# Reciprocal roots by bits and Newton steps on VectorE in a two-layer decoder, in place of ScalarE's square root

## The chip, the cores and the metric

The kernel runs on one core of a Trainium2 chip. Its time is the device time of that core in microseconds (us), the median of several executions. One further execution is recorded by the hardware profiler; all durations of single instructions come from there.

The engines are called PE (TensorE, matrix products), DVE (VectorE), ACT (ScalarE, functions from tables), POOL (GpSimd) and SP (SyncE, which here only issues transfers). Each works through its own queue of instructions in order.

## The reference

The input x has 4 batches of 512 tokens of 256 channels (2,048 tokens). Two layers follow one another, and each sublayer adds its output to x. What matters here:

- Layer 0: a layer norm, a causal convolution of four taps, then a mixer with 16 heads. Its query/key values are multiplied by a decay and a cosine of position, and divided by `max(sqrt(sum(qk * qk)), 1e-12)`, the sum going over a head's channels for each token; gated values are accumulated over the tokens (a running sum), multiplied back, projected, and layer-normed once more. Then cross-attention over the second input `ctx_768` with 16 heads, then a gate that chooses experts for each token, and the experts.
- Layer 1: an element-wise gated recurrence, a cross-attention block whose linear maps are quantised to whole numbers by maxima over the whole tensor, and a feed-forward part.

Every layer norm is `(x - mean) / sqrt(var + 1e-5)` over 256 channels. The reciprocal square root of that variance, and that of the head norms, are what the change touches.

## The kernel before, in words

A tile is 128 tokens; a batch has 4 tiles (QT = 4), and work goes batch by batch (b = 0 to 3). The kernel has two paths, chosen by what the data are; one runs, and the other stays behind a branch. The executed path goes through these stages:

- `l0_mixers`: the mixer of layer 0 and its cross-attention, interleaved. For a batch the mixer's steps are `normalize` (layer norm), `mix` (the convolution, L743 to L746), `measure` (query/key products, copies and squares on ACT at L756 and L758, sums), `scale`, `scale_near` and `scale_far` (the head norms), `factor` (fetch the factors for one group of heads), `gated_values`, `recall` (L821 is its end on DVE), `emit` (the projection `o`) and `absorb` (the second norm, and the addition to x). The cross-attention runs in 16 units, four a batch; a unit has eight `exponents`: PE makes scores, DVE takes maxima (L914), ACT makes the exponents (L917), which `gather` multiplies with the values. In the course of a batch's units the mixer's steps of the next batch are woven in.
- `l0_gate`, `l0_experts`: the choice of experts and the experts.
- `l1_attn`, `l1_xattn` (fuse, then the hidden block), `l1_ffn`: layer 1. `fold` products of weights for the last stage are put among the earlier ones, and its products `y` end the kernel.

What sets the order: a framework plans the instructions of every engine from the order in which the program gives them and from what each depends on, and it may put one ahead of another on the same engine; it adds the semaphores. What is given through `pinned` (matmuls, L579) or `move` (transfers on SP, L586) keeps the order of the program. Buffers come from pools with a fixed number for each name; a step whose buffer is still in use waits.

ACT holds one table of functions at a time. Where the next function is not in it, a table load (`ACT_TABLE_LOAD` in the profile) stands before the instruction, and is listed under its line.

The places that the change and the steps of the prediction touch:

- `rstd` (L154 to L168): the reciprocal root for the layer norms, on a tile of 128 partitions x 4 values. It adds the epsilon on DVE (L158), takes the root on ACT (L160), inverts on DVE (L162), and does one Newton step on DVE (L164 to L168). `normed` calls it, and so do `absorb` and the norms of the other stages: 28 times on the executed path (four each in `normalize`, the cross-attention's `tokens`, `absorb`, the gate, layer 1's recurrence, its fuse block and its feed-forward part).
- `scale_near` (L777 to L785): the head norms of a batch, laid out as 128 x 64: maximum with 1e-24 on DVE (L781), root on ACT (L782), reciprocal on DVE (L783), and two products with `near_dec` (L784, L785). Four times. Its input is fetched by SP from a buffer in memory (`rn<-far_ss`), its output goes back there (`far<-rn`), and from there to `factors`.
- `cosines` (L702 to L717): angles on DVE (L708 to L712), sine and square on ACT (L714, L715), and the product with the decays on POOL (L716, L717). The decays are powers built by doubling on DVE (L680 to L682), stored, and fetched again by SP as `near_dec` (used at L687 to L690) and as `decay`.
- The queue of SP at the start holds, in this order: weights and x, `far_dec<-dec` (2), `near_dec<-far_dec` (2), `decay<-far_dec` (16), `far_ss<-sums`, `rn<-far_ss`, `far<-rn` (2), `factors<-far`.

Of the kernel before, what the change touches and what calls it, by code (L numbers as in the profile page):

```python
# [9 lines left out]
F32 = mybir.dt.float32  # L10
F32R = mybir.dt.float32r
BF16 = mybir.dt.bfloat16
I32 = mybir.dt.int32
AF = mybir.ActivationFunctionType
ALU = mybir.AluOpType
# [3 lines left out]
P = 128  # L19
# [7 lines left out]
EPS = 1e-5  # L27
# [5 lines left out]
TWO_PI_INV = 0.15915494309189535  # L33

MAGIC = 12582912.0
FLT_MAX = 3.4028234663852886e38
CLAMP = 10000.0


class Kernel:  # L40


    def __init__(self, ctx, tc, a, out):
# [30 lines left out]
        self.magic = self.const.tile([P, 1], F32, name="magic")  # L74
        nc.gpsimd.memset(self.magic, MAGIC)

# [74 lines left out]
        return self.ps2.tile([P, 2, 512], F32, tag="pair", name=name)  # L151


    def rstd(self, var, n, pool):  # L154

        nc = self.nc
        v = pool.tile([P, n], F32, tag="ln_v", name="ln_v")
        nc.vector.tensor_scalar_add(v, var, EPS)  # L158
        s = pool.tile([P, n], F32, tag="ln_s", name="ln_s")
        nc.scalar.activation(s, v, AF.Sqrt)  # L160
        y = pool.tile([P, n], F32, tag="ln_y", name="ln_y")
        nc.vector.reciprocal(y, s)  # L162
        u = pool.tile([P, n], F32, tag="ln_u", name="ln_u")
        nc.vector.tensor_mul(u, y, y)  # L164
        nc.vector.tensor_mul(u, u, v)
        nc.vector.tensor_scalar(u, u, -0.5, 1.5, ALU.mult, ALU.add)
        r = pool.tile([P, n], F32, tag="ln_r", name="ln_r")
        nc.vector.tensor_mul(r, y, u)  # L168
        return r

    def moments(self, srcs, pool):

# [366 lines left out]
def l0_mixers(k):  # L539
# [18 lines left out]
    nc, tc, a = k.nc, k.tc, k.a  # L558
    k.close_psum()
    with ExitStack() as es:  # L560
        pool = lambda n, bufs, **kw: es.enter_context(tc.tile_pool(name=n, bufs=bufs, **kw))
        wp, wk, sp = pool("l0_w", 1), pool("l0", 2), pool("l0_s", 3)
# [214 lines left out]
        def scale_near(b):  # L777
            rn = near_of[b] = wk.tile([P, 3, 64], F32, tag="rn", name=f"rn_{b}", bufs=1)
            move(rn[:, 2, :], near(factors[b]))

            nc.vector.tensor_scalar_max(rn[:, 2, :], rn[:, 2, :], 1e-24)  # L781
            nc.scalar.activation(rn[:, 2, :], rn[:, 2, :], AF.Sqrt)  # L782
            nc.vector.reciprocal(rn[:, 2, :], rn[:, 2, :])  # L783
            nc.vector.tensor_mul(rn[:, 0, :], rn[:, 2, :], near_dec[:, 1, :])  # L784
            nc.vector.tensor_mul(rn[:, 1, :], rn[:, 2, :], near_dec[:, 0, :])  # L785

# [321 lines left out]
        for u in range(units + 1):  # L1108
            b, m = divmod(u, 4)
# [927 lines left out]
```

## Time and profile before

| | before |
|---|---|
| median of 3 runs | 1335.3 us (1335.01 to 1341.83) |
| profiled execution | 1344.59 us, span 1342.9 us |
| mean granted clock of PE | 0.847 of full speed |
| instructions | 11,723 |
| PE busy | 1002.3 us, 75% of the span |
| PE weight loads (beside PE) | 550.3 us, 41% |
| DVE busy | 789.0 us, 59%, 1,813 instructions |
| ACT busy | 454.5 us, 34%, 748 instructions |
| POOL busy | 205.5 us, 15% |

Busy time by stretch of the span, in us, as the trace gives it:

| stretch | work in it | PE | DVE | ACT | POOL |
|---|---|---|---|---|---|
| 0 to 32 | first norm, convolution, query/key | 15.9 | 16.7 | 8.1 | 9.0 |
| 32 to 62 | cosines, decays, head norms of batch 0 | 25.3 | 20.3 | 14.1 | 12.9 |
| 62 to 100 | factors of batch 0, `recall` | 10.0 | 20.7 | 4.1 | 9.6 |
| 100 to 157 | first units | 56.2 | 29.2 | 21.1 | 6.8 |
| 157 to 555 | layer 0's mixer and cross-attention | 287.6 | 277.5 | 228.3 | 62.4 |
| 555 to 900 | gate, experts, folds | 259.8 | 146.5 | 52.2 | 60.5 |
| 900 to 1105 | layer 1's recurrence, first part of its cross-attention | 147.5 | 117.9 | 64.9 | 42.2 |
| 1105 to 1343 | hidden block, feed-forward part | 200.1 | 160.3 | 61.9 | 2.3 |

An engine's busy time tells how much work it has; whether it holds others up is seen from the waits. A group of instructions is listed as line, engine, operation, what it writes and reads with the shape, and how often; after a bar its busy time and the mean duration of one in ns; after another the idle time of its engine before it and what ended most of that. The timeline lists single instructions by their start.

### The profile page before, as it was taken

To read this page: it belongs to the slowest core of one execution; us is meant where nothing else is said; L and a number is where in the kernel's file an instruction comes from. 1 tells how busy PE (TensorE), PEld (TensorE's weight loads), DVE (VectorE), ACT (ScalarE), POOL (GpSimd) and SP (SyncE) were. 2 spreads that over 40 slices of the span, in tenths; PEclk is the share of its full clock that TensorE was granted. 3 is DMA by queue.
4 is the path that set the end of the run, shared out by engine and by line. 5 is a ranking of instruction groups with operands and counts; after the bars stand their busy time and mean duration, and the time that the engine had idled before them with its cause. 6 is when DMAs were issued, how large, how long until landed. Compare 5 with 4: busy or idle time off the path is not lost. (4 is left out here: it accounts for less than half of the span.)

```text
span 1342.9 us, 11723 instructions
## 1 busy us (share of the span) xinstructions
PE 1002.3 (75%) x3734; PEld 550.3 (41%) x3734; DVE 789.0 (59%) x1813; ACT 454.5 (34%) x748; POOL 205.5 (15%) x224
## 2 busy tenths in 40 slices
PE   5729759767956867467199999948883688769997
PEld 1315332232413313156077577836442344245443
DVE  5565577578587666345136851145565656886564
ACT  2404437537555565310011421102341344741000
POOL 2321012112112101015300000071113110000000
PEclk9859869868977878766599999979996899878999
DMA  4264722343541322044575354173000011001000
GB/s 131 69 186 153 239 70 95 120 132 103 169 143 58 117 72 69 19 148 146 175 260 164 110 206 130 50 247 127 0 0 4 17 47 32 0 28 36 16 31 19
DMA packets 92344, 132.27 MB, mean 98 GB/s; under 512 B 21312, under 2 KB 62784, under 8 KB 92256
## 3 DMA queue, kind: packets, MB, share of 16 engines
q1 hardware_dynamic: 86768, 113.58, 27.0%
q0 software_dynamic: 5504, 17.83, 3.7%
q8 instruction: 32, 0.52, 0.2%
q14 instruction: 40, 0.33, 0.1%
HBM read 88.72 MB, written 42.66 MB: 98 GB/s over the span
## 5 line engine op out<-in xcount | busy, mean ns | idle before, releaser
L917 ACT ACTIVATE e<-score,tops 128x512 f32<-128x512 f32 x256 | 161.3, 687 | 144.1 <-DVE tops L914 79.9
L914 DVE TENSOR_REDUCE tops<-score 128x2 f32<-128x1024 f32 x128 | 155.5, 1219 | 61.9 <-PE score L579 61.7
L210 PE MATMUL y<-folded_sb,fht 128*128 128x512 f32 x256 | 113.4, 604 | 0.0
L952 PE MATMUL av<-e,weighed 128*32 128x512 f32 x512 | 86.0, 742 | 33.1 <-POOL weighed L940 33.1
L579 PE MATMUL score<-query,key 64*128 64x512 f32 x256 | 75.2, 586 | 43.7 <-ACT e L917 43.2
L1893 DVE SCALAR_TENSOR_TENSOR x_sb<-y,tt_w,x_sb 128x256 f32<-128x256 f32 x128 | 61.9, 483 | 39.2 <-PE y L210 35.9
L579 PEld LDWEIGHTS score<-query,key 64*128 64x128 f32 x256 | 27.7, 214 | 136.6 <-ACT e L917 83.9
L210 PE MATMUL ef<-sw,eact 128*128 128x256 f32 x320 | 80.2, 391 | 1.6 <-DVE ey L1411 1.6
L579 PE MATMUL o<-o_wT_sb,qk 128*128 128x256 f32 x128 | 43.2, 494 | 49.1 <-DVE qk L821 39.6
L210 PE MATMUL ef<-eht,sw 128*128 128x320 f32 x256 | 74.6, 435 | 0.6 <-ACT eact L1400 0.6
L210 PEld LDWEIGHTS y<-folded_sb,fht 128*128 128x128 f32 x256 | 49.3, 194 | 60.4 <-issue 60.4
L210 PE MATMUL fold<-w_out,w_in 128*128 128x256 f32 x256 | 69.7, 432 | 5.5 <-DMA w_out<-in_w_outT 5.5
L210 PEld LDWEIGHTS ef<-sw,eact 128*128 128x128 f32 x320 | 59.3, 195 | 12.5 <-DVE ey L1411 4.9
L210 PEld LDWEIGHTS fold<-w_out,w_in 128*128 128x128 f32 x256 | 55.1, 221 | 14.3 <-issue 5.9
L210 PEld LDWEIGHTS ef<-eht,sw 128*128 128x128 f32 x256 | 47.6, 190 | 18.4 <-ACT eact L1400 1.6
L579 PEld LDWEIGHTS o<-o_wT_sb,qk 128*128 128x128 f32 x128 | 30.0, 248 | 61.2 <-DVE qk L821 44.9
L1400 ACT ACTIVATE eact<-ef 128x640 f32<-128x640 f32 x32 | 22.4, 703 | 94.8 <-PE ef L210 94.7
L579 PE MATMUL xo<-Wo_sb,att 128*128 128x256 f32 x128 | 37.0, 438 | 16.8 <-POOL att L993 16.8
L210 PE MATMUL f<-aht,W_fT_sb 128*128 128x512 f32 x96 | 45.8, 620 | 2.8 <-DVE up L1511 1.4
L940 POOL TENSOR_TENSOR weighed<-v,weighed 128x256 f32<-128x256 f32 x16 | 10.9, 682 | 237.7 <-ACT weighed L939 237.7
L1435 POOL DMA_INDIRECT got<-table,rows x32 | 31.1, 972 | 105.1 <-DMA table<-ey 94.1
L1380 PE MATMUL eturn<-ident,rows 128*128 128x128 f32 x80 | 16.6, 291 | 34.7 <-DMA rows<-table 30.7
(372 smaller groups left out, 1803.8 us busy)
## 6 DMA issues: line engine op xcount, KB each, us to landing
table<-zeros POOLq DMA_DIRECT2D x8, 1152.0 KB
factors<-far SPq DMA_DIRECT2D x64, 128.0 KB
key<-far_k SPq DMA_DIRECT2D x16, 512.0 KB
query<-far_q SPq DMA_DIRECT2D x16, 512.0 KB
w_in<-in_w_in SPq DMA_DIRECT2D x8, 1024.0 KB
w_out<-in_w_outT SPq DMA_DIRECT2D x8, 1024.0 KB
rows<-table SPq DMA_DIRECT2D x8, 640.0 KB
table<-ey SPq DMA_DIRECT2D x8, 640.0 KB
```

The costliest lines, as they stand in the source:

```text
L210: self.nc.tensor.matmul(out, lhs_t, rhs, start=(i == 0), stop=(i == len(pairs) - 1))
L579: nc.tensor.matmul(out, lhs_t, rhs, start=start and i == 0, stop=stop and i == len(pairs) - 1)
L914: nc.vector.tensor_reduce(top, ps, AX.X, ALU.max, negate=True)
L917: nc.scalar.activation(e[:, i, :], ps[:, i, :], AF.Exp, bias=top[:, i : i + 1])
L940: weighing[0] = nc.gpsimd.tensor_mul(wt[:, :, :, 0:16], vs[u], wt[:, :, :, 16:17].to_broadcast([P, QT, 4, 16]),)
L952: nc.tensor.matmul(avs[u][32 * h : 32 * h + 32, :], weighed[u % 2][:, j, h, :], es_of[u, h // 2, j][:, h % 2, :], start=(j == 0), stop=(j ...
L1380: nc.tensor.transpose(ps[:, c, :], rows[:, i, c * P : (c + 1) * P], k.ident)
L1400: nc.scalar.activation(act[:, f, :].rearrange("p (j t) -> p j t", j=2), ps[:, :, :half], AF.Silu)
L1435: nc.gpsimd.indirect_dma_start(out=got, out_offset=None, in_=k.table, in_offset=bass.IndirectOffsetOnAxis(ap=k.rows[:, which, t : t + 1], ...
L1893: nc.vector.scalar_tensor_tensor(xt, ps[:, e, :], w[:, i, e4 + e : e4 + e + 1], xt, ALU.mult, ALU.add)
```

## The change

`rstd` no longer calls ACT. It computes half of (variance + epsilon) in one DVE instruction and hands it to a new helper, `inverse_root`. This takes a first guess from the bits of the float: one DVE instruction reads the half as a whole number, multiplies by -0.5 and adds a constant, and writes the whole number whose bits are the guess. The constant sets the sign bit too, so that the guess is negative. Three Newton steps follow, of three DVE instructions each: y times y, times the half, and (u - 1.5) times y, which flips the sign each time, so that after three steps it is positive. `rstd` has thus 11 DVE instructions in place of 6 and one on ACT.

`scale_near` does the same on its 128 x 64 tile: half of the maximum with 1e-24, then `inverse_root` in place, 11 DVE instructions in place of a maximum, ACT's root and a reciprocal. The two products with `near_dec` stay. Two small tiles are new.

```diff
+ROOT_BITS = float(0x5F3759DF - (1 << 22) - (1 << 31))

+    def inverse_root(self, y, half, u):
+        nc = self.nc
+        nc.vector.tensor_scalar(y.bitcast(I32), half.bitcast(I32), -0.5, ROOT_BITS, ALU.mult, ALU.add)
+        for _ in range(3):
+            nc.vector.tensor_mul(u, y, y)
+            nc.vector.tensor_mul(u, u, half)
+            nc.vector.scalar_tensor_tensor(y, u, 1.5, y, ALU.subtract, ALU.mult)
+
     def rstd(self, var, n, pool):
-        nc = self.nc
-        v = pool.tile([P, n], F32, tag="ln_v", name="ln_v")
-        nc.vector.tensor_scalar_add(v, var, EPS)
-        s = pool.tile([P, n], F32, tag="ln_s", name="ln_s")
-        nc.scalar.activation(s, v, AF.Sqrt)
-        y = pool.tile([P, n], F32, tag="ln_y", name="ln_y")
-        nc.vector.reciprocal(y, s)
-        u = pool.tile([P, n], F32, tag="ln_u", name="ln_u")
-        nc.vector.tensor_mul(u, y, y)
-        nc.vector.tensor_mul(u, u, v)
-        nc.vector.tensor_scalar(u, u, -0.5, 1.5, ALU.mult, ALU.add)
-        r = pool.tile([P, n], F32, tag="ln_r", name="ln_r")
-        nc.vector.tensor_mul(r, y, u)
-        return r
+        half, y, u = (pool.tile([P, n], F32, tag=f"ln_{t}", name=f"ln_{t}") for t in ("half", "y", "u"))
+        self.nc.vector.tensor_scalar(half, var, EPS, 0.5, ALU.add, ALU.mult)
+        self.inverse_root(y, half, u)
+        return y

     def scale_near(b):
-            nc.vector.tensor_scalar_max(rn[:, 2, :], rn[:, 2, :], 1e-24)
-            nc.scalar.activation(rn[:, 2, :], rn[:, 2, :], AF.Sqrt)
-            nc.vector.reciprocal(rn[:, 2, :], rn[:, 2, :])
+            half, u = (sp.tile([P, 64], F32, tag=f"rn_{t}", name=f"rn_{t}_{b}", bufs=1) for t in ("half", "u"))
+            nc.vector.tensor_scalar(half, rn[:, 2, :], 1e-24, 0.5, ALU.max, ALU.mult)
+            k.inverse_root(rn[:, 2, :], half, u)
             nc.vector.tensor_mul(rn[:, 0, :], rn[:, 2, :], near_dec[:, 1, :])
             nc.vector.tensor_mul(rn[:, 1, :], rn[:, 2, :], near_dec[:, 0, :])
```

## The prediction

> **What bounds the kernel now.** I read the page's busy shares first: PE 75%, VectorE (DVE) 59%, ScalarE (ACT) 34%. No engine is full over the span, so a price has to be looked up stage by stage. The change touches ACT and DVE, so the groups of instructions come next.
>
> ```profile
> L160 ACT ACT_TABLE_LOAD x20 | 25.7, 1283 | 1.1 <-PEq L2018 0.8
> L917 ACT ACT_TABLE_LOAD x12 | 15.4, 1283 | 3.5 <-PE av L952 2.5 <-DVE tops L914 0.8
> L160 ACT ACTIVATE ln_s<-ln_v 128x4 f32<-128x4 f32 x28 | 5.8, 205 | 53.8 <-DVE ln_v L158 40.3 <-issue 13.3
> L782 ACT ACT_TABLE_LOAD x3 | 3.8, 1283 | 0.1
> ```
>
> Columns after the bars: busy us and mean ns of one; idle time before and who ended it. Each root costs 0.2 us, but a table load of 1.283 us stands in front of most of them, and another in front of the next `Exp` (L917). ACT runs 48 loads in all, 61.6 us of its 454.5.
>
> Then the waits, to see where ACT is late for others:
>
> ```profile
> PEld score L579 <- ACT e L917: 83.9, 67, 5.3
> ACT e L917 <- DVE tops L914: 79.9, 56, 16.0
> DVE tops L914 <- PE score L579: 61.7, 65, 3.6
> PE o L579 <- DVE qk L821: 39.6, 9, 10.7
> ```
>
> Columns: us in total, times, longest. In layer-0 attention (157 to 555 us), PE's scores wait for ACT's exponents, those for DVE's maxima, and those for PE: a ring in which now one engine, now another is last. A us taken from ACT is not a us of the span.
>
> Last, the timeline at the start and at two roots inside the ring (start us, length, engine, line, operation, idle before and its releaser):
>
> ```profile
> 32.05 0.21 ACT L160 ACTIVATE ln_s<-ln_v 128x4 f32<-128x4 f32 x1
> 32.29 0.18 DVE L162 RECIPROCAL ln_y<-ln_s 128x4 f32<-128x4 f32 x1 [8.76 <-ACT ln_s L160]
> 37.27 1.28 ACT L714 ACT_TABLE_LOAD   x1 [5.01 <-DVE ang L712]
> ...
> 23.54 25.90 SPq L586 DMA_DIRECT2D decay<-far_dec  x16
> 49.55 0.36 SPq L586 DMA_DIRECT2D far_ss<-sums  x1
> 51.44 0.34 SPq L586 DMA_DIRECT2D rn<-far_ss  x1
> ...
> 95.73 4.52 PE L579 MATMUL o<-o_wT_sb,qk 128*128 128x256 f32 x11 [3.94 <-DVE qk L821]
> ```
>
> ```profile
> 237.10 0.26 ACT L782 ACTIVATE rn<-rn 128x64 f32<-128x64 f32 x1 [0.53 <-DVE rn L781]
> 237.38 1.28 ACT L917 ACT_TABLE_LOAD   x1
> ...
> 239.99 0.80 PE L579 MATMUL score<-query,key 64*128 64x512 f32 x2 [4.94 <-ACT e L917]
> ...
> 428.43 0.16 DVE L164 TENSOR_TENSOR ln_u<-ln_y 128x4 f32<-128x4 f32 x1
> 428.63 0.16 DVE L165 TENSOR_TENSOR ln_u<-ln_u,ln_v 128x4 f32<-128x4 f32 x1
> 428.82 0.17 DVE L166 TENSOR_SCALAR ln_u<-ln_u 128x4 f32<-128x4 f32 x1
> ```
>
> At the start, DVE stands 8.76 us behind one 0.2 us root, queued on ACT behind copies and squares. At 237 the root and its load hold the exponents, and PE waits 4.94 us. From 428.43 I read the price of the new work: dependent small DVE operations start 0.20 us apart. Where the queue interleaves other work, only their busy 0.16 us counts.
>
> **What the Trainium skill says.** "ScalarE: Activation LUTs", What ACT_TABLE_LOAD costs: about 1283 ns for every set, plus a drain of about 1380 ns. The first agrees (1283); the second does not appear here: at 237.10 the load starts 0.02 us after the root ends. So I price a switch at 1.283. "VectorE: DVE Perf Modes", Rules for kernel authors: chained operations aren't cheaper for being fused, the count of them matters. The 0.20 us step agrees, and I count instructions. "SBUF — State Buffer", on the shared port pair: a DVE operation with two SBUF inputs blocks against a GpSimd (POOL) operation that reads SBUF. The trace has such a case: an L165 multiply, 246 ns on average, took 1.14 us at 434 us under POOL's L993. The new chains hold 9 such operations each in place of 3.
>
> **The change, part by part.** Sums are against the profiled execution, 1344.6 us, span 1342.9; the median of the runs is 1335.3, 9.3 below it. I carry a difference from one to the other unscaled.
>
> *ACT.* 32 roots go: 28 x 0.205 + 4 x 0.257 = 6.8 us. With no root on ACT, the tables wanted on the executed path are the sine, then tanh and exponent, sigmoid and silu by stage; in the built order 8 loads remain of 48: 40 x 1.283 = 51.3 us. ACT falls from 454 to about 396. Of this, 24 loads and 12 roots (33.3 us) lie in the ring from 157 to 555 us.
>
> *DVE.* `rstd` goes from 6 instructions to 11, `scale_near` from 4 to 13: 28 x 5 + 4 x 9 = 176 more. 140 x 0.16 = 22.4. For the 128x64 ones no row shows the new forms; the multiplies L784/L785 (0.22 to 0.23) stand in: 4 x (11 x 0.22 - 0.20 - 0.54) = 6.7. Sum 29 us busy, DVE 789 to 818. `scalar_tensor_tensor` and the integer-typed guess at these sizes are in no row: between 0.16 and 0.3 each, 128 instructions, so 0 to 18 us more busy. I take 0.16 for the four-column ones.
>
> *The start (gain 8, range 4 to 10).* Today the second batch's `normalize` waits 8.76 us for ACT's root. New: 11 x 0.20 = 2.2 us on DVE, no wait, so the angles (L708 to L712) come about 6.5 earlier, minus what the chain takes in between them. ACT's sine waits 5.01 for them. The cosines free the buffers for the last of the 16 decay transfers, which SP issues from 23.5 to 49.4; behind these in SP's queue stand far_ss (49.55) and rn (51.44). If they go with the angles, far_ss leaves about 6 earlier. Then the near factors: from L781 at 57.0 to the issue of far at 61.3 is 4.3 us with the load; new 13 x 0.2 = 2.6. So far can leave about 8 earlier, then factors, `recall`, and PE's `o` at 95.7, from which PE is busy 56.15 of the next 57 us. All that is late moves whole. It is 4 if the transfers themselves limit: the 16 engines are 61% busy from 62 to 100 us.
>
> *The ring (gain 6, from -5 to +20).* Twelve places, each a load, a root and a load back, 2.8 us. Read by hand: at 237 PE waits for it: 2.5. At 217 the maxima wait 1.30 for the root: 1.5. At 466 and 540 ACT's exponents were late by one load each: 1.3 + 1.3. At 346 DVE has just been waited for: 0. The seven others stand where DVE goes from maximum to maximum without a gap (it is busy 31.9 of the 43 us from 157 to 200, and 26.4 of 30 from 410 to 440): 0 to 2, I take 0.7, and each pays five more DVE operations, 0.7. That is 6.6 + 7 x 0 = 6.6, less 0.8 for a port stall or so: 6.
>
> *Later (loss 2.5).* There ACT has slack (52 of 345 us busy between 555 and 900), so a load saved is worth nothing: they stand before an idle ACT, the one at 877.43 runs 13 us ahead of its root. DVE's longer chain shows where a layer norm heads a stage: gate +0.5, the start of layer-1 attention (916 to 925, three norms in a row) +0.7, its turns +0.3, the hidden block's norm near 1031 +0.5, the last block +0.5. Elsewhere PE hides it, above all from 1105 on (200 of 238 us).
>
> *Moved.* SP's transfers keep their order. PE: 16 fold matmuls move ahead of the first turn of layer-1 attention, about 16 x 0.43 = 7 us of work that has to be done anyway and that its slack absorbs; turns and their products are interleaved differently in two batches. DVE: the last decay powers (L680 to L682) stand ahead of the first conv work (L746), which delays PE's first `qk` by some 1.5 us, in turn covered by the sums' copy, which comes only at 40.67; the near decays' steps (L687 to L690) stand inside the second norm, before the angles, and would wait there for their transfer (issued at 22.67) if it were late: up to 2 us of the start's 8; in the second unit of a batch one maximum ahead of `absorb`'s updates. POOL: some cosine steps swap. At nothing each, under PE's backlog; at 1 us each if that cover is gone.
>
> Sum: -8 - 6 + 2.5 = -11.5; span 1331.4, median about 1323.8. The unpriced gain at places where I took 0.7 leans further down, so 1323.
>
> **Rivals.** *ACT is the ring's bound.* For: 127 us of PE's score waits (83.9 + 43.2, overlapping) end on ACT. Against: ACT is busy 81 of 155 us from 255 to 410, itself waiting 79.9 for maxima. If most of the 33 counts, plus 8: gain 25 to 38, 1297 to 1310. *Hidden.* The start is bound by the transfers (4) and the ring gives nothing back: 4 - 2.5, within 0.5%, 1329 to 1341. *DVE becomes the bound, slower.* Place: the units with `absorb` and the next batch's mixing (192 to 220, 410 to 440), and norms that head a stage. Price: 140 operations x 0.20 dependent + 4 x 9 x 0.25 = 37 us if all stand on the path, plus port stalls of 1 to 2. It decides when over some 27 of these 37 are exposed, against the start's 8 and the ring's 12 before its DVE price, with 6.7 for the half per cent: then 1342 to 1350. Against: most norms are interleaved with maxima or lie under PE. *The change doesn't do what it says*: loads stay, because tanh, exponent and sigmoid alternate anyway. The built order, 8 loads, speaks against; it would end in the hidden case.
>
> **How the numbers follow.** Mine (gain 7 to 20): 0.46. ACT bound (over 20): 0.24. Hidden: 0.21, loads staying included. Slower: 0.09. What can be told from no change here is about 0.5%, 6.7 us. Faster 0.70, same 0.21, slower 0.09. Range 1303 to 1338: it leaves out part of the ACT-bound case (0.08) and the slower one with the hidden one's upper edge (0.11). Mine alone: 1315 to 1328.
>
> **What would show it.** ACT's loads 8 and its busy time near 396; DVE near 818 (over 830: the new forms are dearer). Start: DVE's 8.76 us wait gone, far_ss issued near 43, the long run of PE from near 88 rather than 96. Ring: its end (the last `e` of L917, near 555) earlier than the start's shift by about 6; if by 20 or more, ACT was its bound; if by nothing, DVE was. Later stages: each some tenths longer. I am wrong if the start's transfers don't move with the angles, or if the chain's DVE work meets POOL's port often.

## The result: no gain

Timed beside the kernel before, with 20 runs each, the changed kernel took 1344.16 us (1337.70 to 1349.19) against 1337.1 (1333.89 to 1342.09): ratio 1.0042, 95% interval 1.0027 to 1.0058. Two repeats in later sets gave 1.0012 (0.9995 to 1.0029) and 0.9994 (0.9973 to 1.0016). So it is between no change and 0.4% slower. The forecast, 1323 and at most 1338, was wrong. Its profiled execution took 1347.23 us, span 1345.5, 2.6 us more than the span before. The first profile of the kernel before (1344.59) lies above all 20 of its runs here, 7.5 us above their median, so leads over it are kinder than the medians.

Line numbers of the changed kernel are 2 higher behind `rstd` (its L203 was L201); in `rstd` and its helper, L169 makes the half, L160 the guess, L162 to L164 are a Newton step.

The page's busy row, and from the groups of ACT two of the seven rows of table loads that are left:

```profile
PE 1009.1 (75%) x3734; PEld 551.9 (41%) x3734; DVE 822.3 (61%) x1989; ACT 399.4 (30%) x676; POOL 206.0 (15%) x224
```

```profile
L1234 ACT ACT_TABLE_LOAD x2 | 2.6, 1283 | 0.0
...
L716 ACT ACT_TABLE_LOAD x1 | 1.3, 1283 | 0.2 <-DVE ang L714 0.2
```

The other five rows have one load each: eight loads, 55 us less on ACT, 33 us more on DVE: the change did what it says, and the span did not shrink. Where ACT waited for a load or a root, another engine's lateness now ends the wait, as the waits of the changed kernel show (total us, times, longest; PEld is PE's weight loads):

```profile
ACT e L919 <- DVE tops L916: 93.0, 61, 15.7
...
PEld score L581 <- ACT e L919: 69.1, 56, 5.3
...
DVE tops L916 <- PE score L581: 51.0, 59, 4.2
```

PE waits for ACT 15 us less than before (69.1 for 83.9), and ACT waits for DVE 13 us more (93.0 for 79.9). In the ring of layer 0, DVE took over most of the place that ACT gave up.

**The lead along the span.** The best view for such a change is one that no single row gives: the start of the same DVE instruction in both traces. The table gives the lead of each profiled execution over the first profile of the kernel before (median over DVE instructions within 6 us of the place; positive is earlier; the last column is the difference of the spans). Two traces of the same kernel drift apart too: the one of the kernel before taken later loses some 7 us between 500 and 960. So a step of a few us counts only where several kernels show it, or where the trace shows its instructions.

| at (us of before) | 220 | 245 | 400 | 500 | 840 | 960 | 1060 | 1160 | end |
|---|---|---|---|---|---|---|---|---|---|
| changed kernel | 8.0 | 13.1 | 14.2 | 9.1 | 11.2 | 11.8 | 3.4 | -2.2 | -2.6 |
| the same, repeat (e5) | 7.4 | 12.3 | 13.0 | 9.7 | 12.2 | 12.7 | 7.0 | 2.1 | 1.7 |
| the same, repeat (e14) | 8.5 | 13.8 | 14.7 | 9.6 | 9.1 | 9.0 | 3.4 | -1.7 | -2.1 |
| kernel before again (e13) | 1.3 | 1.1 | 1.2 | 0.9 | -1.6 | -5.7 | -5.8 | -5.9 | -6.2 |
| layer 1 old (e1) | 8.9 | 13.8 | 14.6 | 11.1 | 11.2 | 13.3 | 13.5 | 10.7 | 10.5 |
| only layer 1 new (e2) | 0.0 | 0.1 | 0.1 | -0.2 | -2.6 | -4.9 | -11.8 | -17.7 | -18.0 |
| only fuse block new (e15) | 1.1 | 1.0 | 1.0 | 1.0 | 1.2 | -2.5 | -7.7 | -13.0 | -13.4 |
| two Newton steps (e7) | 8.6 | 14.4 | 15.7 | 12.6 | 15.4 | 17.3 | 14.3 | 8.9 | 12.5 |
| mixer's first and head norms new (e16) | 7.7 | 13.3 | 13.0 | 13.3 | 14.0 | 16.1 | 16.3 | 16.8 | 16.5 |
| ring's other norms new (e17) | 4.2 | 5.1 | 6.2 | 1.8 | 5.4 | 8.3 | 8.5 | 2.1 | 2.0 |
| ring's other and fuse norms old (e18) | 9.5 | 15.3 | 14.5 | 14.6 | 17.1 | 16.3 | 15.0 | 15.0 | 14.3 |

The changed kernel leads by 8 after the start, by 13 after the head norms at 237, loses 5 between 400 and 500, and 14 after 960. The four places, one after the other:

**The start.** Timeline of the changed kernel (start, length, engine, line, operation, idle before and its releaser):

```profile
30.63 0.43 DVE L711 TENSOR_SCALAR turns<-ang 128x512 f32<-128x512 f32 x1 [2.06 <-PE ss L581]
...
33.03 0.61 ACT L760 ACTIVATE sq<-qk 128x512 f32<-128x512 f32 x1
...
33.88 1.28 ACT L716 ACT_TABLE_LOAD   x1 [0.25 <-DVE ang L714]
...
45.74 0.36 SPq L588 DMA_DIRECT2D far_ss<-sums  x1
...
47.52 0.34 SPq L588 DMA_DIRECT2D rn<-far_ss  x1
...
54.87 1.20 SPq L588 DMA_DIRECT2D far<-rn  x2
...
87.19 7.70 PE L581 MATMUL o<-o_wT_sb,qk 128*128 128x256 f32 x26 [3.94 <-DVE qk L823]
```

The 8.76 us behind the root are gone. The sine's load waits 0.25 us for the angles in place of 5.01. It starts 3.4 us earlier and not 5, since ACT's last square in front of it ends at 33.64 where it ended at 32.17: the convolution now stands behind the last decay powers, and query/key come later. `far_ss` moves by 3.8 us. From the first DVE operation of the head norms to the issue of `far` it is 4.1 us (50.74 to 54.87), hardly less than the 4.3 before. But this work starts 3.2 us after the fetch of `rn` is issued, and before 5.6 (51.44 to 57.04), where DVE stood 2.75 us at a gated product that waited for PE. So the head norms leave at 54.87 rather than 61.31, and PE's long run begins 8.5 us earlier. The 2 us between these two leads go with the second group of factors, which SP issues in 6.4 us in place of 9.0.

**The head norms of the next batch**, at 237 before, some 10 us earlier now. PE in the changed kernel:

```profile
228.46 0.50 PE L581 MATMUL score<-query,key 64*128 64x512 f32 x2 [1.44 <-ACT e L919]
228.89 1.98 PE L581 MATMUL g<-xc,g_wT_sb 128*128 128x512 f32 x4
230.71 1.88 PE L581 MATMUL v<-xc,v_wT_sb 128*128 128x512 f32 x4
```

The same `g` products in the kernel before:

```profile
240.72 3.78 PE L579 MATMUL g<-xc,g_wT_sb 128*128 128x512 f32 x4
```

PE waits 1.44 us there in place of 4.94: 3.5 us. The rest is PE's granted clock, its share of full speed: behind the long wait the kernel before had 0.50 (239.9 to 244.6), and the changed kernel has 1.00 (228.4 to 230.9). The two scores, four `g` and four `v` take 4.1 us up to the next score in place of 7.1. PE is 6.6 us further ahead behind them; on DVE the step at 245 is 5.1.

**The third batch of the ring, 410 to 430.** VectorE and then POOL in the changed kernel:

```profile
413.80 1.03 DVE L169 TENSOR_SCALAR ln_half<-ln_mv 128x4 f32<-128x4 f32 x1
...
415.08 0.98 DVE L160 TENSOR_SCALAR ln_y<-ln_half 128x4 int32<-128x4 int32 x1
...
424.14 1.19 DVE L162 TENSOR_TENSOR ln_u<-ln_y 128x4 f32<-128x4 f32 x1
425.37 1.19 DVE L163 TENSOR_TENSOR ln_u<-ln_u,ln_half 128x4 f32<-128x4 f32 x1
...
426.67 1.22 DVE L916 TENSOR_REDUCE tops<-score 128x2 f32<-128x1024 f32 x1
```

```profile
413.54 2.49 POOL L995 TENSOR_TENSOR att<-att,shares 128x512 f32<-128x512 f32 x2 [7.28 <-DMA shares<-far_inverse]
...
424.05 2.49 POOL L995 TENSOR_TENSOR att<-att,shares 128x512 f32<-128x512 f32 x2
```

Six chain operations of two norms (two more at 422.74 and 423.45, of 0.68 and 0.66) take 5.7 us where they take 6 x 0.16 elsewhere: 4.8 us of stall while POOL works. From 422.74 to 426.59 DVE does nothing but the chain, and the maximum (L916) for which the exponents wait comes behind it. In the kernel before one operation was stalled at this place, by 1 us:

```profile
434.03 1.14 DVE L165 TENSOR_TENSOR ln_u<-ln_u,ln_v 128x4 f32<-128x4 f32 x1
```

**Layer 1.** The fuse block's norm of a batch is not done when that block begins: the built order weaves it into the recurrence of the next batch, three times. PE in the kernel before and in the changed one, over the first such batch (its `f` products begin at 955.22 and at 943.45):

```profile
962.25 1.73 PE L201 MATMUL turn<-ident,h 128*128 128x128 f32 x8
964.48 0.70 PE L210 MATMUL down<-W_downT_sb,state 128*128 128x256 f32 x2 [0.49 <-DVE up L1511]
...
968.41 1.88 PE L210 MATMUL f<-aht,W_fT_sb 128*128 128x512 f32 x4
971.12 4.58 PE L210 MATMUL down<-W_downT_sb,state 128*128 128x256 f32 x20 [0.83 <-DVE state L1514]
```

```profile
951.61 0.70 PE L212 MATMUL down<-W_downT_sb,state 128*128 128x256 f32 x2 [1.02 <-DVE up L1513]
952.14 0.60 PE L203 MATMUL turn<-ident,h 128*128 128x128 f32 x4
955.20 1.22 PE L212 MATMUL down<-W_downT_sb,state 128*128 128x256 f32 x2 [2.45 <-DVE state L1516]
...
957.06 4.86 PE L212 MATMUL f<-aht,W_fT_sb 128*128 128x512 f32 x6
961.76 4.48 PE L212 MATMUL down<-W_downT_sb,state 128*128 128x256 f32 x20
```

Before, the norm's eight turns stand ahead of the first `down` pair, and the next six `f` products fill PE's waits for the scan in two portions; the long run of `down` starts as the last scan ends (wait 0.83 <-DVE state). In the changed kernel the norm is done later, four turns stand behind each of the first two `down` pairs, PE waits 2.45 us for a scan with the six `f` queued behind it, and these then stand ahead of the long run. The last scan ends 17.7 us after the batch's addition to x, where it was 17.1. The long run, which is late by 2.4 (19.6 after the addition, before 17.2), waits for PE and no longer for the scan.

And the six `f` take 4.9 us in place of 3.0. The windows over them (stretch, then busy time of PE, its weight loads, DVE, ACT and POOL, and the granted clock as the third number from the right), in the kernel before, in the changed one for the first and second batch, and in its repeat e5 (see the experiments) for the second:

```profile
968.30:970.40 2.10, 1.99 (x6) 0.66 (x4) 0.66 (x2) 0.00 (x0) 1.27 (x1) 1.00 0.00 0
```

```profile
957.00:962.00 5.00, 5.00 (x10) 2.15 (x9) 1.38 (x2) 0.00 (x0) 1.26 (x1) 0.57 0.00 0
980.60:985.40 4.80, 4.80 (x7) 2.02 (x6) 1.57 (x2) 0.00 (x0) 1.26 (x1) 0.52 0.01 3
```

```profile
979.70:982.90 3.20, 3.20 (x8) 1.40 (x7) 1.55 (x2) 0.00 (x0) 1.26 (x1) 0.81 0.02 5
```

In the kernel before PE has the full clock there, in the changed one little over half. In the second batch the repeat, the same program in the same order, has 0.81: its `f` take 3.33 us instead of 5.01, and its batch 22.1 instead of 23.7. So the order with its longer chain costs something at the better clock too (0.9 us here), and more where the clock is low.

From one batch's addition to x (`x_sb<-x_sb,down`) to the next takes 24.1, 23.7 and 24.4 us; before, 21.8, 21.2 and 23.3: 5.9 us. In the repeats e5 and e14 it is 24.1, 22.1 and 23.5, so 3.5 us; the first profile is the dearest of three. With the repeat's 3.3 us for the six `f` twice, and the last batch's run of `down` at 6.6 as before and not 7.2, it would be some 2 us: by this estimate about 4 of the 5.9 go with the clock. The last of the three spacings says least, since e1 and e11, one program, show 22.7 and 24.1 there. Then the last batch's norm heads the fuse block, with POOL adding a bias to x at the same time (L1773, 1018.64 to 1025.58). The changed kernel's DVE there, and then that of the kernel before:

```profile
1021.51 1.79 DVE L160 TENSOR_SCALAR ln_y<-ln_half 128x4 int32<-128x4 int32 x1
...
1023.81 1.78 DVE L162 TENSOR_TENSOR ln_u<-ln_y 128x4 f32<-128x4 f32 x1
```

```profile
1025.91 0.71 DVE L158 TENSOR_SCALAR ln_v<-ln_mv 128x4 f32<-128x4 f32 x1
...
1028.98 2.24 DVE L164 TENSOR_TENSOR ln_u<-ln_y 128x4 f32<-128x4 f32 x1
```

With one more of 0.92 (L169, 1020.08) the changed chain loses some 4.0 us to stalls, the old one 2.6. From the last addition to the end of the last maximum over the text (`txt_tops`) is 18.0 us, before 15.9: another 2.1. This stretch is called the head of the fuse block below. And at 1141 eight products of attention run slower than before (3.70 us):

```profile
1141.54 5.72 PE L212 MATMUL bav<-bet,keys 128*128 128x512 f32 x8 [0.68 <-ACT bet L1811]
```

PE's granted clock is 0.79 there (1132.5 to 1149.0), and was 1.00 (1133 to 1147). From 1060 to 1160, the stretch of these products and those before them, the lead falls by 5.6 us. That this part comes from the new norms is not shown: e9 and e17, described below, lose 5.3 and 6.4 us there, and all their norms of layer 1 have the old form.

### The profile page after: what moved, and what is told of

Same layout as the page of the kernel before. It is cut to its first block, busy times and chain, and to the rows that moved or that the text cites. A ratio compares the mean times of both kernels' runs of the same rounds, so it can differ in the third digit from the quotient of the medians.

```text
span 1345.5 us, 11829 instructions
## 1 busy us (share of the span) xinstructions
PE 1009.1 (75%) x3734; PEld 551.9 (41%) x3734; DVE 822.3 (61%) x1989; ACT 399.4 (30%) x676; POOL 206.0 (15%) x224
## 5 line engine op out<-in xcount | busy, mean ns | idle before, releaser
L916 DVE TENSOR_REDUCE tops<-score 128x2 f32<-128x1024 f32 x128 | 155.6, 1220 | 51.3 <-PE score L581 51.0
L954 PE MATMUL av<-e,weighed 128*32 128x512 f32 x512 | 88.7, 765 | 26.6 <-POOL weighed L942 26.6
L581 PEld LDWEIGHTS score<-query,key 64*128 64x128 f32 x256 | 27.8, 214 | 131.7 <-ACT e L919 69.1
L212 PE MATMUL fold<-w_out,w_in 128*128 128x256 f32 x256 | 66.6, 418 | 5.2 <-issue 5.2
L212 PEld LDWEIGHTS fold<-w_out,w_in 128*128 128x128 f32 x256 | 53.1, 213 | 13.3 <-issue 5.5
L212 PE MATMUL f<-aht,W_fT_sb 128*128 128x512 f32 x96 | 49.7, 668 | 1.4 <-DVE x_sb L1521 1.4
L581 PE MATMUL xo<-Wo_sb,att 128*128 128x256 f32 x128 | 37.1, 439 | 17.1 <-POOL att L995 17.1
L942 POOL TENSOR_TENSOR weighed<-v,weighed 128x256 f32<-128x256 f32 x16 | 10.6, 663 | 229.9 <-ACT weighed L941 229.9
L203 PE MATMUL turn<-ident,h 128*128 128x128 f32 x96 | 19.1, 342 | 34.5 <-DVE h L190 33.8
## 6 DMA issues: line engine op xcount, KB each, us to landing
w_out<-in_w_outT SPq DMA_DIRECT2D x8, 1024.0 KB, 12.6
```

What stands on the lines that cost most here:

```text
L203: nc.tensor.transpose(ps[:, i * P : (i + 1) * P], h[:, i, c * P : (c + 1) * P], self.ident)
L212: self.nc.tensor.matmul(out, lhs_t, rhs, start=(i == 0), stop=(i == len(pairs) - 1))
L581: nc.tensor.matmul(out, lhs_t, rhs, start=start and i == 0, stop=stop and i == len(pairs) - 1)
L916: nc.vector.tensor_reduce(top, ps, AX.X, ALU.max, negate=True)
L942: weighing[0] = nc.gpsimd.tensor_mul(wt[:, :, :, 0:16], vs[u], wt[:, :, :, 16:17].to_broadcast([P, QT, 4, 16]),)
L954: nc.tensor.matmul(avs[u][32 * h : 32 * h + 32, :], weighed[u % 2][:, j, h, :], es_of[u, h // 2, j][:, h % 2, :], start=(j == 0), stop=(j ...
```

## Experiments

A *set* is the kernels that ran together; they share the runs of the kernel before. That kernel took 1337 to 1339 us in three sets (the first comparison; e5 to e8; e17 and e18) and 1349 to 1351 in the other three, with ranges of 8 to 17 us in each. Its runs in the sets with 1349 to 1351 show a mean granted clock of 0.844, in those of e5 and e17 0.847 and 0.848; what makes the difference is not settled. So ratios are compared within a set, and traces across sets by their steps.

In the mixed kernels `rstd` returns the form of the kernel before where a flag is set; everything else is as in the changed kernel.

```diff
     def rstd(self, var, n, pool):
+        if self.old:
+            return self.rstd_old(var, n, pool)
...
+            k.old = True
             h = k.layer_norm(b)
+            k.old = False
```

### Which layer, which norms

**e1**, flag at the three norms of layer 1 (12 of 28 `rstd`); **e2**, the kernel before with only these 12 new; **e3**, flag at the fuse block's norm alone (4); **e4**, flag at the recurrence's norm alone (4).

> Changed kernel, but the 12 norms of layer 1 (recurrence, fuse block, feed-forward) keep the ScalarE root. Theory A (what layer 0 gains is lost again in layer 1, by the new form there): layer 0 keeps the 11.2 us that it is ahead at 840 us in the changed kernel's trace, and nothing is given back: about 1337 - 11 = 1326 us, ratio 0.992. Theory B (the granted clock takes the gain back, whatever the form of the norms in layer 1): the lead at 840 us is there, but is lost by the end: 1334 to 1342 us, ratio near 1.

> Kernel before, but the 12 norms of layer 1 take the new form (the other 16 norms and the head norms keep the ScalarE root). Theory A: no lead at 840 us, then 4.8 us lost in the recurrence, 3.3 at the head of the fuse block and about 1 at the feed-forward: +9, 1346 us, ratio 1.007. Theory B: within 3 us of the kernel before.

> Changed kernel, but the 4 norms of the fuse block keep the ScalarE root. In the built order this puts the turns of the recurrence's next batch ahead of its down products again, as before, though the recurrence's own norms have the new form. If the order is what costs the 4.8 us of the recurrence: its batches follow 21.5 us apart as before (not 24), and with the 3.3 us of the fuse block the time is about 1344 - 8 = 1336 us. If the longer VectorE chain costs them: batches still 24 us apart, about 1344 - 3 = 1341 us.

> Changed kernel, but the 4 norms of the recurrence in layer 1 keep the ScalarE root. In the built order the turns stay behind the first down product, as in the changed kernel. If the order costs the 4.8 us: batches still 24 us apart, 1342 to 1345 us. If the longer VectorE chain costs them: 21.5 us apart, about 1344 - 5 = 1339 us.

Measured, beside 1351.14 of the kernel before:

| | us | ratio (95%) | additions to x, apart | head of fuse block | last `bav` x8 |
|---|---|---|---|---|---|
| kernel before (first profile) | | | 21.8, 21.2, 23.3 | 15.9 | 3.70 |
| changed kernel (first profile) | | | 24.1, 23.7, 24.4 | 18.0 | 5.72 |
| e1 layer 1 old | 1336.49 | 0.9889 (0.9861 to 0.9917) | 21.8, 21.2, 22.7 | 16.1 | 3.70 |
| e2 only layer 1 new | 1356.80 | 1.0040 (1.0023 to 1.0057) | 23.1, 23.3, 24.3 | 18.0 | 5.53 |
| e3 fuse block old | 1339.60 | 0.9912 (0.9883 to 0.9942) | 21.8, 21.2, 23.2 | 16.2 | 3.70 |
| e4 recurrence old | 1344.73 | 0.9948 (0.9930 to 0.9966) | 23.7, 23.4, 24.4 | 18.0 | 5.75 |

The loss is in layer 1, and it goes with the four norms of the fuse block: with these old (e3), the spacing, the head and the products are those of the kernel before, though recurrence and feed-forward part have the new form. The recurrence's own four norms change none of the three (e4). e4's ratio below one says little here, since the kernel before took 1351 in this set; beside e3, in the same set, it is 5.1 us slower.

**e15** turns e3 round: the kernel before with only the fuse block's four norms new. **e11** repeats e1.

> Kernel before with the new form in the fuse block's 4 norms alone. If they are what loses after 900 us: the recurrence's second to fourth additions to x come 23 to 24 us apart (21.8 and 21.2 before), the stretch from the last of them to the last text maximum takes 18.0 us (15.9 before), 6 to 8 us lost in all: ratio 1.004 to 1.006. If it takes the new form elsewhere too (the recurrence's own norms, a changed order before them): within 2 us of before.

> Changed kernel with the ScalarE root in layer 1's 12 norms once more, on the chip of the others. By the traces it ends 10.4 us ahead of the kernel before, the changed kernel 1.7 us ahead to 2.6 us behind: ratio 0.992. If the first figure (0.989) holds on this chip too: 0.987 to 0.991. If the granted clock takes the lead back here: over 0.996.

e15 took 1355.48 us, ratio 1.0039 (1.0015 to 1.0063). It starts even with the kernel before, and everything comes after 840: additions 22.5, 22.6 and 24.1 us apart, head 18.0, the slow `bav`, 14.6 us of lead lost from 840 to the end. The kernel before, traced in the same set (e13), loses 4.6 us over this stretch with nothing changed, so about 10 are left. Four norms of the 32 roots are enough for the late loss in the recurrence and at the head; for the part after 1060 see the slow `bav` below. e11 took 1334.57 against 1349.05, ratio 0.9880 (0.9847 to 0.9913), as e1.

### Length of the chain

**e6** is the kernel before with its chains made as long as the new ones, by dependent multiplications by one; all roots and loads stay. **e7** is the changed kernel with two Newton steps, 8 operations in place of 11 (the third step is left out). **e12** is e7 with layer 1's norms old.

```diff
         nc.vector.tensor_mul(r, y, u)
+        for _ in range(5):
+            nc.vector.tensor_mul(r, r, self.ones[:, :n])
...
             nc.vector.reciprocal(rn[:, 2, :], rn[:, 2, :])
+            for _ in range(9):
+                nc.vector.tensor_mul(rn[:, 2, :], rn[:, 2, :], k.ones[:, :64])
```

```diff
-ROOT_BITS = float(0x5F3759DF - (1 << 22) - (1 << 31))
+ROOT_BITS = float(0x5F3759DF - (1 << 22))
...
-        for _ in range(3):
+        for _ in range(2):
```

> Kernel before with its ScalarE roots, and behind each layer norm's root five dependent multiplications by one on VectorE (128x4), behind each head norm's nine (128x64): the change's 176 additional VectorE instructions without what it removes. Theory A (the longer chain and the order that follows from it cost about 14 us after 840 us): slower by some 10 us or more in layer 1, and by what the ring pays in layer 0: 1.007 to 1.02. If the extra instructions are hidden and something else is at fault: within 0.4%.

> The changed kernel with two Newton steps in place of three (the third step is left out, so that the roots are less exact): 3 instructions fewer in each of the 32 roots. In the built order the turns of the recurrence stay behind the first down product. If the order makes the cost: the recurrence's batches still 24 us apart, and only the fuse block's head and the crowded third batch of layer 0 gain, 2 to 4 us in all. If the number of dependent instructions makes it: 96 fewer, of which those on the path at 0.2 us each, 6 to 10 us.

> The new form with two Newton steps (the third is left out) in layer 0, the ScalarE root in layer 1. With two steps the lead at 840 us was 15.4 us against 11.2 to 12.2 with three; with layer 1 as before nothing of it should be lost: 1339 - 15 = 1324 us, ratio 0.988, the fastest of all that compute the whole. If the lead is capped by other work: no better than the same kernel with three steps, 0.991 to 0.993.

e6: 1359.93 us against 1339.41, ratio 1.0144 (1.0121 to 1.0167). A chain made longer, with all else kept in the program, costs some 20 us here; in the changed kernel the removed roots and loads, and the other order, set about as much against it. Its recurrence keeps nearly the order of the kernel before: six or eight turns ahead of the first `down`, the `f` in portions, four of them in 1.9 us. There the chain only delays the turns by 1.0 and the last scan by 0.8 to 1.0, and the additions are 22.6, 22.2 and 23.8 us apart. Its head is 17.0, its last `bav` slow.

e7: 1332.09, ratio 0.9950 (0.9932 to 0.9967); three operations fewer in each chain bring it from even (e5, in the same set) to 0.5% faster. It has the new order too: its additions are 22.6, 21.5 and 23.5 apart, with the six `f` ahead of the long run of `down` in both of the first two, in 4.54 us at a clock of 0.62 and in 2.84 us at 1.00. Its head is 17.4, and between 400 and 500 it loses 3.1 us of its lead where the changed kernel loses 5.1. e12: 1335.68 against 1349.05, 0.9898 (0.9862 to 0.9933), no better than e11 beside it, although e12 has the shorter chain in layer 0.

So in the recurrence length alone costs 0.5 to 1.0 us a batch (e6). The rest of the changed kernel's 2.3 and 2.5 in the first two goes with the order and its slower `f`; but e7, with this order and a shorter chain, loses only 0.8 and, in the second batch with its full clock, 0.2. How order and chain length share in it, apart from the clock, is not separated.

### POOL at the head of the fuse block

**e8**, the changed kernel, and **e9**, the kernel before, without POOL's addition of the bias to x in the fuse block (which is left out of the result).

```diff
-            nc.gpsimd.tensor_add(xb, xb, b_f2[:, None, :].to_broadcast([P, QT, D]))
```

> The changed kernel without GpSimd's addition of the second bias to x beside the fuse block's norms (this addition is left out). In the changed kernel's trace three VectorE instructions of a norm's chain took 0.92, 1.79 and 1.78 us there, while GpSimd worked on it. If these stalls carry the 3.3 us that the head of the fuse block loses: it wins back 2 to 4 us. If the chain's own length does: within 1 us of the changed kernel.

> Control to the changed kernel without GpSimd's bias addition beside the fuse block's norms: the kernel before without the same addition (left out). Taking it out of the changed kernel brought its fuse block's head 6.6 us forward and 16 us in the median. If that is the port stalls of the new chain: here it brings at most the one stall of the old chain and the addition's own place on the path, 1 to 4 us (0.997 to 0.999). If the addition itself is what is on the path, whatever the form of the norms: about as much as in the changed kernel, 0.988 to 0.992.

e8: 1326.07 us, ratio 0.9909 (0.9892 to 0.9927); head 14.0, `bav` 3.70. e9: 1341.91, ratio 0.9942 (0.9922 to 0.9961); head 13.2, `bav` slow. With the addition the stalls of this chain go too: its operations take 0.15 to 0.17 us in both, so it is POOL's work that stalls them. But the addition is on the path with either form of the norm: without it the lead grows from 1000 to 1060 by 6.2 us in e8 and by 6.9 in e9. So the 16 us between e8 and e5 in one set are not the price of stalls of the new form. What the new form loses by the addition is the difference of the heads: 18.0 - 15.9 = 2.1 us with it, 14.0 - 13.2 = 0.8 without, so 1.3.

On the slow `bav`: among the kernels that keep POOL's addition, all with a head of 17.0 to 18.0 us have it (the changed kernel, e2, e4, e5, e6, e7, e14, e15). With a head of 15.9 to 16.2 nine traces don't (the kernel before, e1, e3, e10, e11, e12, e13, e16, e18), but e17 does: its norms of layer 1 are all old, its head is 16.1, and its `bav` takes 5.63 us. Without the addition e8, new form, is fast, and e9, old form, is slow. So neither the new instructions nor a long head is needed for it, and the 5 to 6 us between 1060 and 1160 can't be put down to the change. Repeats of one program agree; what lowers the clock is not shown.

### What in layer 0 is worth having

**e10** and, in another set, **e16** are the same kernel: only the mixer's first norm (`normalize`) and the head norms new, 8 of the 32 roots. **e17** has only the ring's other norms (`tokens`, `absorb`) new. **e18** is the changed kernel with these and the fuse block's old.

```diff
+    old = True
...
         def normalize(b):
+            k.old = False
             normal[b] = k.layer_norm(b)
+            k.old = True
```

> Kernel before, with the new form in the mixer's first norm (4 of the 32 roots; the second of them stands in front of the cosines) and in the head norms (4), the ScalarE root everywhere else. By the prediction's step on the start: far_ss is issued about 4 to 6 us earlier and PE's projection of batch 0 starts about 8 us earlier, and this lead reaches the end: 1331 us where before is 1339, ratio 0.994. The ring's table loads for the other norms remain, so if the ring's gain came from loads, this kernel has only part of it; if the lead at the start is taken back in the ring by its order, ratio 0.998 to 1.002.

> The kernel before with the new form in the mixer's first norm and the head norms alone, once more: its trace was 15.3 us ahead at 560 us and 8.6 at the end. If its lead holds in every set: ratio 0.988 to 0.993. If the figure of 0.990 came from a slow set of the kernel before: 0.994 to 0.997 beside a kernel before of 1338.

> Kernel before, with the new form in absorb's norm and the cross-attention's tokens norm alone (8 of 32 roots). By the sum of the prediction these are most of the ring's loads: a gain of 2 to 4 us by 560 us, ratio 0.997 to 0.999. By the theory formed since (their loads were hidden, their longer chain stalls in the crowded third batch): nothing gained up to 400 us, 4 to 5 us lost between 400 and 440 us, ratio 1.002 to 1.005.

> Changed kernel with the ScalarE root kept in the two places that lose: the 8 norms of absorb and tokens, and the 4 of the fuse block. If what was lost is lost there and nowhere else: the lead of 13 to 15 us at 400 us reaches the end, ratio 0.988 to 0.992, as with the first norm and the head norms alone. If the other new norms (gate, recurrence, feed-forward) lose something too: 0.993 or more.

| | us | kernel before beside it | ratio (95%) |
|---|---|---|---|
| e10 | 1336.14 | 1349.05 | 0.9901 (0.9864 to 0.9938) |
| e16 | 1332.84 | 1349.84 | 0.9895 (0.9860 to 0.9930) |
| e17 | 1346.00 | 1338.93 | 1.0043 (1.0028 to 1.0058) |
| e18 | 1330.39 | 1338.93 | 0.9944 (0.9921 to 0.9966) |

e10 and e16 have the whole gain: their lead is 13 to 15 us from 245 to 500, and nothing is lost in the third batch (e16 ends with 16.5 us, e10 with 8.7). The groups of ACT in e16 show what they kept (in its listing L183 is the old root, L942 the exponent):

```profile
L183 ACT ACT_TABLE_LOAD x18 | 23.1, 1283 | 0.3
L942 ACT ACT_TABLE_LOAD x9 | 11.5, 1283 | 3.4 <-PE av L977 2.5 <-DVE tops L939 0.8
```

With the other rows 40 of the 48 loads are still there (51.3 us), ACT is busy 442.5 us, and the kernel is as far ahead at 245 as the changed one, and further at 500. With the ring's other eight roots new (e17) 12 loads go, the lead is 6.2 us at 400, and 4.4 of it are lost by 500. It loses 6.4 more between 1060 and 1160, where it has no new instruction, and its median is 0.4% slower: by themselves these roots are worth nothing. e18 confirms both places at once: without the ring's other norms and the fuse block's, the changed kernel keeps its lead up to 840 (17.1) and most of it to the end (14.3).

Within their sets e16 beats the kernel before and the changed one (e14) by 1%, e10 the kernel before by 1%, and e18 the kernel before by 0.6%. Against the sets where the kernel before took 1337 to 1339, 1333 to 1336 would be 0.1 to 0.5%. Which of e16 and e18 is better was not compared in one set.

### Repeats

**e5** and **e14** are the changed kernel again, **e13** is the kernel before as if it were a change.

> The changed kernel once more, to stand beside the others on one chip. If the parts add up (layer 0 in the new form 0.989, layer 1 in the new form 1.004): about 0.993 of the kernel before. If the two parts make each other worse, or the first measurement holds here too: 1.003 to 1.006. In the trace, if the granted clock fell between 1110 and 1150 us by chance, the eight bav products that took 5.7 us (3.7 before) take 3.7 now; if it belongs to the new form of the fuse block's norms (three traces with it show 5.5 to 5.75, three without it 3.70), they take 5.5 again.

> The kernel before itself, traced once more: ratio 1. In its first trace PE's clock held between 1110 and 1150 us (eight bav products in 3.70 us). If the fall of the clock there comes and goes with any kernel, this trace may show 5.5 to 5.75 us instead, and its time is then some 4 us more than the first trace's; if it is bound to kernels that differ from the kernel before, 3.70 again.

> The changed kernel a third time. If the sets in which the kernel before takes 1350 slow it alone: 1342 to 1344 us again, whatever the kernel before takes, so a ratio of 0.994 to 0.996 in such a set and 1.001 to 1.004 in the others. If such a set slows all kernels: 1.001 to 1.004 in both.

e5: 1342.01 against 1339.41, ratio 1.0012 (0.9995 to 1.0029). e14: 1348.51 against 1349.84, 0.9994 (0.9973 to 1.0016). e13: 1350.01 against 1349.84, 0.9992 (0.9973 to 1.0010), so a ratio within a set can be trusted to about 0.2%. Its trace loses 2.7 us in the experts and 4 more by 960 against the first trace of the same kernel, with nothing changed. From one kind of set to the other the changed kernel follows the kernel before up (1342 to 1344, 1348.5), while e1, e10, e11, e12 and e16 stay at 1333 to 1337 (e3 at 1340) in sets where the kernel before took 1349 to 1351. Why is open.

## Why the prediction was wrong

Its sum, against the lead of the first profile of the changed kernel:

| step | predicted | measured |
|---|---|---|
| the start (lead at 157) | 8 | 6.9 |
| the root at 217 (157 to 220) | 1.5 | 1.1 |
| head norms at 237 (220 to 245) | 2.5 | 5.1 |
| the rest of the ring (245 to 545, lead there 8.9) | 2.0 | -4.2 |
| gate, experts (545 to 840) | -0.5 | 2.3 |
| recurrence, head of the fuse block (840 to 1060) | -1.5 | -7.8 |
| hidden block to the end (from 1060) | -0.5 | -6.0 |
| sum | 11.5 | -2.6 |

- **The start** came out near the forecast in size, in part by luck. I let the sine go with the angles; it stood behind ACT's squares, which came 1.5 us later because of the moved decay powers. The prediction had named these and put them at nothing, "in turn covered by the sums' copy". So far_ss moved by 3.8 us, to 45.74 and not 43. For the head norms "new 13 x 0.2 = 2.6" measured 4.1, against 4.3 before. That far left 6.4 us earlier all the same comes from DVE, which reached this work sooner; that was in no step.
- **The head norms at 237**: right and too small. I counted 2.5; PE's wait fell by 3.5, since two loads had stood in it (235.30 and 237.38), and PE's full clock behind the shorter wait gave 3 more.
- **The rest of the ring** fell. The singles at 466 and 540 were not there: the changed kernel's lead doesn't grow from 455 (9.5) to 545 (8.9), and e16, which keeps these roots and loads, loses nothing to it. "The seven others ... 0 to 2, I take 0.7, and each pays five more DVE operations, 0.7", less "0.8 for a port stall or so", was the term with the wrong size: in the third batch alone 5 us, from six stalls. I had named 410 to 440 as a place of the slower rival and read DVE as full there, but priced five more operations at 0.7, where stalls make a single one up to 1.2.
- **Later, "loss 2.5"** is the step that failed: after 840 it had 2.0, and 13.8 were measured. Of these, 7.8 lie before 1060. For the recurrence it had only "the start of layer-1 attention (916 to 925, three norms in a row) +0.7, its turns +0.3". The norms that stand among the recurrence's work (in the trace before near 958, 980 and 1001) are the fuse block's, and it is these and not the recurrence's own that cost 3 to 6 us there (e3, e4, e15). **"At nothing each, under PE's backlog"** was wrong with it: in the recurrence PE has no backlog, it waits for scans, and turns put behind a `down` push the `f` products in front of the next `down`. I had listed that turns and products are interleaved differently "in two batches", and put no price on it. By the estimate above about 2 us of the 5.9 are this order and the longer chain, about 4 PE's lower clock in it, which I had in no step. What it called "the hidden block's norm near 1031 +0.5" is the fuse block's last, and measured 2.1. The other 6.0 us, nearly all between 1060 and 1160, go with PE's clock. They were in no step either, and their cause stays open: e9 and e17 lose as much there with the old norms.
- **The counts** were right: 8 loads, ACT 399.4 for 396, DVE 822.3 for 818.
- **The rivals**: ACT was not the ring's bound (e10 and e16 against the changed kernel; no 20 us). It ended between the hidden case and the slower one, by the mechanism of the slower, and by PE's clock, which no rival had: the places were those named (410 to 440, and norms that head a stage), the stalls on POOL's port those named as what would make me wrong. I gave that 0.09, since I looked for cover by PE for the average norm, and did not ask of each of the seven kinds of norm what runs beside it.

## What to carry to other kernels

A table load is worth removing where an engine stands waiting for it: 8 of 32 roots held all the gain that lasted here, and a kernel that keeps 40 of the 48 loads is faster than one that keeps 8. What replaces a load on another engine has to be priced at each place by what runs beside it there: a chain of 11 small dependent DVE operations is 2.2 us alone (6.56 to 8.74 in the changed kernel), and beside POOL operations stalls added 4.0 us to one chain at the head of the fuse block and 4.8 to two in the third batch. And for a norm that is woven into another stage, find in the built order whose work it stands among, and what its move pushes in front of the product that is waited for.

## What the hardware showed beyond that

- The stalls under POOL are not confined to operations with two inputs. The Trainium skill, "SBUF — State Buffer", SBUF: two separate sides, lets a DVE operation meet a GpSimd one in the shared ports when it has two SBUF inputs or runs in a two-port mode. L169 and L160 read one tensor, and took 1.03 and 0.92 (L169), 0.98 and 1.79 us (L160) while POOL worked, against 0.17 elsewhere. That agrees if they run in such a mode, which no run here shows.
- A small integer operation on a float's bits costs DVE no more than a float one here: the guess took 0.17 us where nothing disturbed it, on 128x4, and 194 ns on average on 128x64, as the float operations beside it (L169 0.17) and before it (L781 0.19).
- PE's granted clock is part of the cost of an order of instructions. With the same 3,734 matmuls PE is busy 991.8 us in e16, 1002.3 in the kernel before, 1009.1 in the changed one and 1012.4 in e15. Six `f` products took 3.0 us at 1.00 and 4.9 to 5.0 at 0.52 to 0.57; eight `bav` 3.70 or 5.5 to 6.1 (6.14 in e9, without POOL's addition); four `g` 1.98 at 1.00 and 3.78 at 0.50. PE's waits shortly before were longer in some of the slow cases (2.45 us for the scan), but the second batch of the changed kernel and of e5, with the same waits, ran at 0.52 and 0.81. No run here tells what sets it.
